# Layer 0 attention: the state behind each sequence's last chunk, and its part of the transposed k, are left out

## The chip, the cores and the metric

The kernel runs on one core of a Trainium2 chip. The metric is the device time of one execution in microseconds. Besides the timed runs there is one execution recorded by the hardware profiler; all durations below come from that recording, and its own time stands in the table further down.

A core has five engines that run beside each other and wait for each other by semaphores: TensorE (PE in the profile, with its weight loads shown apart as PEld), VectorE (DVE), ScalarE (ACT), GpSimd (POOL) and SyncE (SP), which here issues DMAs. PSUM is the memory that PE writes its results to.

## What is computed

Two blocks follow one another, each of the form x + attention(xn) * silu(ffn(xn)), on x of shape (4, 1024, 512), with xn = layernorm(x). The change is in the attention of layer 0, a linear attention with a decay per head. It runs over chunks of a sequence and carries a state S of 32 x 32 per head from chunk to chunk:

```python
def body(S, xs):
    qb, kb, vb = xs
    scores = jnp.einsum('bhid,bhjd->bhij', qb, kb) * intra_decay[None]
    o_intra = jnp.einsum('bhij,bhjd->bhid', scores, vb)
    o_inter = jnp.einsum('bhid,bhde->bhie', qb * q_decay[None, :, :, None], S)
    S_new = blk_decay[None, :, None, None] * S + jnp.einsum('bhjd,bhje->bhde', kb * k_decay[None, :, :, None], vb)
    return (S_new, o_intra + o_inter)
S0 = jnp.zeros((B, H, d, d), dtype=q.dtype)
_, o = jax.lax.scan(body, S0, (qc, kc, vc))
```

The output of a chunk reads the state in front of it (`S`). The scan's final state is thrown away (`_`). The remaining parts, which are the feed-forward network of layer 0 with ternary weights, a softmax attention with rotary positions in layer 1 and a gated feed-forward network, are not touched.

## The kernel before

The 4096 rows are eight blocks of 512 (`BLK`), so a sequence of 1024 rows is an even block and the odd block behind it. A block is four chunks of 128 rows (`TPB` = 4, `P` = 128; the kernel's chunk is twice the reference's), and the 16 heads are four groups of four heads, 128 columns each. The layer 0 attention goes through 32 steps, one for each block and group, in this order: block 0 groups 0 to 3, block 1 groups 0 to 3, and so on.

For a block and group these helpers do the work:

- `project` (matmul on L350): kT and qT, that is k and q with the group's 128 columns on the partitions and the block's 512 rows along the free axis. ACT copies each out of PSUM and adds the bias (L355), and POOL multiplies qT with its decay into qd (L357).
- `turn_k`: transposes kT chunk by chunk on PE into the PSUM tile k0t (L367), which DVE multiplies with k's decay into kd (L369).
- `states`: one matmul for each chunk, kd of the chunk with v of the chunk, into the PSUM tile u (L382). DVE copies it with a mask, which keeps the four heads apart, into slots 1 to 4 of `state[g]` (L390), and then adds to each slot the decayed slot in front of it (L395). Slot i is the state in front of chunk i. In an even block slot 0 is zero and isn't used; in an odd block POOL first copies slot 4, which the even block left, to slot 0 (L389).
- `scores`: 32 small matmuls into two large PSUM tiles sc (L408), which DVE multiplies with the decay into pt (L416).
- `outs`: state slots times qd (L432) and v times pt (L439), into the PSUM tile o, which ACT copies to oT (L445). It reads slots 0 to 3 (1 to 3 in an even block).

In step n the helpers stand on PE in this order: `scores` of step n, `project` of step n+1, a first job, `outs` of step n, `turn_k` of step n+1, in groups 0 and 1 two transposes of normalised rows of the next block (tr_x, L146), a second job, `states` of step n+1. So `turn_k` and `states` of a group are issued one step ahead. The jobs are, in groups 0 and 1, two tiles of the output projection of the block before (wo, L333, with a bias add on DVE, L338), and in groups 2 and 3 two tiles of v of the next block (v0ps, L324, with a bias add on DVE, L328). The second tile of group 3 is the fourth tile of v, which comes directly ahead of `states` of the next block's group 0. In the step before the last there are no jobs, and in the last the jobs turn rows for the feed-forward network (L457).

PE's order is kept as written. DVE, ACT, POOL and SP are ordered by a scheduler that runs when the program is built, apart from single instructions that are pinned. PSUM tiles come from a pool with two buffers for each of three kinds: k0t and tr_x share one kind (`tr`), the results of L350, L324, L333, L382 and `outs` share another (`acc`), and the tiles sc are the third. A buffer is written again when its reader has finished. Also on DVE in this stage are the statistics of the next block's rows (bn_stats and its aggregate, L105 and L108, a copy, L297, reciprocals and products, L305 to L314, with square roots on ACT, L112), and the preparation of the ternary weights (L183, L208, L210), two pieces to a step.

Of the kernel before, what the change touches and what calls it, by code (L numbers as in the profile page):

```python
# [16 lines left out]
ALU = mybir.AluOpType  # L17
AX = mybir.AxisListType

P = 128  # L20
B, N, D = 4, 1024, 512
NT = B * N
H, HD = 16, 32
# [3 lines left out]
TPB = BLK // P  # L27
# [8 lines left out]
def kernel(ctx, tc, ins, out):  # L36
# [15 lines left out]
    def acc(name):  # L52
        return psum.tile([P, 512], F32, tag="acc", name=name)

    def tr(name):
        return psum.tile([P, 4, P], F32, tag="tr", name=name)
# [177 lines left out]
    with ExitStack() as es:  # L234
# [35 lines left out]
        bdmask = wp.tile([P, P], F32, tag="bdmask", name="bdmask")  # L270
# [11 lines left out]
        kdec = wp.tile([P, H], F32, tag="kdec", name="kdec")  # L282
# [58 lines left out]
        def project(blk, g):  # L341
# [18 lines left out]
            )  # L360
            return qT, kT, qd

        def turn_k(blk, g, kT):
            nm = f"{blk}_{g}"
            kps = tr(f"k0t_{nm}")
            for i in range(TPB):
                nc.tensor.transpose(kps[:, i, :], kT[:, i * P : (i + 1) * P], ident)  # L367
            kd = p2.tile([P, TPB, P], F32, tag="kd", name=f"kd0_{nm}", bufs=1)
            nc.vector.tensor_tensor(  # L369
                kd.rearrange("p c (r d) -> p c r d", d=HD),  # L370
                kps.rearrange("p c (r d) -> p c r d", d=HD),
                kdec[:, None, 4 * g : 4 * g + 4, None].to_broadcast([P, TPB, 4, HD]),
                ALU.mult,
            )
            return kd

        def states(blk, g, kd):
            nm = f"{blk}_{g}"
            v = vs[blk]
            u = acc(f"u0_{nm}")  # L380
            for i in range(TPB):
                nc.tensor.matmul(  # L382
                    u[:, i * P : (i + 1) * P], lhsT=kd[:, i, :], rhs=v[:, i, g * P : (g + 1) * P],
                    start=True, stop=True,
                )
            s = state[g]
            fresh = blk % 2 == 0
            if not fresh:
                nc.gpsimd.tensor_copy(s[:, 0, :], s[:, TPB, :])  # L389
            nc.vector.tensor_tensor(  # L390
                s[:, 1:, :], u.rearrange("p (c e) -> p c e", e=P),
                bdmask[:, None, :].to_broadcast([P, TPB, P]), ALU.mult,
            )
            for i in range(1 if fresh else 0, TPB):
                nc.vector.scalar_tensor_tensor(  # L395
                    s[:, i + 1, :], s[:, i, :], blkdec[:, g : g + 1], s[:, i + 1, :],
                    ALU.mult, ALU.add,
                )
# [95 lines left out]
        for i in range(TPB):  # L494
            values(0, i)
        states(0, 0, turn_k(0, 0, cur[1]))
        load_x(1)
        beside = weights0()
        steps = [(blk, g) for blk in range(NBLK) for g in range(4)]
        for n, (blk, g) in enumerate(steps):  # L500
# [19 lines left out]
            if nxt:  # L520
                kd = turn_k(*steps[n + 1], nxt[1])
# [7 lines left out]
            if nxt:  # L529
                states(*steps[n + 1], kd)  # L530
# [15 lines left out]
    with ExitStack() as es:  # L546
# [143 lines left out]
        for g in range(NH0 * NBLK + 2 + 2 * TPB):  # L690
            blk, c = divmod(g, NH0)
# [115 lines left out]
    with ExitStack() as es:  # L807
# [276 lines left out]
        for s in range(TB * nu + LAG + 1):  # L1084
# [4 lines left out]
            e = s - LAG  # L1089
            if s % (2 * TB) == 0 and s < TB * nu:  # L1090

                assert not must
                n = s // (2 * TB) + 1
                if n < 4 * B:
                    b, g = divmod(n, 4)
# [23 lines left out]
            if s < TB * nu:  # L1119
                u, j = divmod(s, TB)  # L1120
# [12 lines left out]
            if 1 <= e <= TB * nu:  # L1133
                u, kb = divmod(e - 1, TB)
# [18 lines left out]
            elif s % TB == (6 if s >= TB * nu else 4) and 0 <= zu < nu - 1:  # L1153
# [3 lines left out]
                b, g, qh = units[zu]  # L1157
# [328 lines left out]
```

## Time and profile before

| what | us |
|---|---|
| median of 3 runs | 3150.0 (3148.52 to 3150.66) |
| the profiled execution | 3149.29 |
| its span, first to last instruction | 3147.5 |
| mean TensorE clock granted over the span | 0.994 of full speed |
| kT x128 transposes (L367), busy on PE | 20.9 |
| u, 128 matmuls in 256 instructions (L382), busy on PE | 35.8 |
| kd x32 (L369), busy on DVE | 22.1 |
| masked copy of u x32 (L390), busy on DVE | 22.1 |
| state updates x112 (L395), busy on DVE | 39.4 |

The layer 0 attention fills the span from its start to about 630 us, where the first matmul of the feed-forward network (L588) begins. A row of a group of instructions gives the source line, the engine, what is written from what, the number of instructions, the busy total, the mean duration of one and the idle time of the engine just ahead of them with the engine and line that ended it. A row of the timeline gives the start and the length of a run of like instructions. The end of a matmul in such a row is modelled, and instructions of one engine may overlap in it, so that the distance from one start to the next is not the duration. In a list of the chain of waits, "issue" is time in which an engine waited for nothing that the profile shows.

### The profile page before, as it was taken

The page shows a single profiled execution, that of the slowest core. Times are in us where ns is not written, and L with a number is a line of the kernel's source. Part 1 is how long each engine was busy: PE and PEld are TensorE (multiplying, and loading weights), DVE is VectorE, ACT ScalarE, POOL GpSimd, SP SyncE. Part 2 cuts the span into 40 slices and gives each one's busy share as a digit, 9 for nine tenths or more (in the row PEclk, how much of TensorE's full clock was granted, in tenths as well). Part 3 has the DMA queues.
Part 4 walks back from the last instruction along what each step waited for, and adds up shares of the span by engine and source line. Part 5 has one row for each costly group of instructions (what it writes and reads, how often), then busy time and mean ns, then how long its engine had stood idle before and what let it go on. Part 6 is the DMA issues. An engine that isn't in the chain of part 4 may idle for free.

```text
span 3147.5 us, 61092 instructions
## 1 busy us (share of the span) xinstructions
PE 3088.4 (98%) x26233; PEld 1765.4 (56%) x26233; DVE 1905.1 (61%) x2638; ACT 1196.1 (38%) x1696; POOL 1501.4 (48%) x615
## 2 busy tenths in 40 slices
PE   9999999999999998999999999999999999999998
PEld 5555555578777874443344444334444435888887
DVE  4444555468888775656656555555555684566655
ACT  3111111155555542444444444444444444333332
POOL 0000000034444344898888988888888970000001
PEclk9999999999999999999999999999999999999999
DMA  3111111122222231100001000010000013322211
GB/s 131 54 54 54 54 57 44 38 64 91 81 81 71 94 138 38 48 9 8 8 17 40 12 12 15 20 35 14 10 17 15 12 44 100 119 75 66 67 51 55
DMA packets 97799, 158.46 MB, mean 50 GB/s; under 512 B 13040, under 2 KB 26864, under 8 KB 97392
## 3 DMA queue, kind: packets, MB, share of 16 engines
q1 hardware_dynamic: 96704, 151.33, 15.5%
q8 instruction: 207, 3.39, 0.5%
q0 software_dynamic: 816, 3.15, 0.3%
q14 instruction: 72, 0.59, 0.1%
HBM read 104.10 MB, written 41.94 MB: 46 GB/s over the span
## 4 chain that ended last, share of the span: by engine, by line
PE 84%; DVE 11%; issue 2%; ACT 2%; POOL 1%; SPq 1%; DMA 0%; ACTq 0%; POOLq 0%; DVEq 0%
PE sk L1027 9%; PE sq L1000 8%; PE y L1046 8%; PE qk L350 7%; PE gate L1218 5%; PE up L1218 5%; PE dn L1240 5%; PE v1ps L856 4%; PE v0ps L324 3%; PE wo L333 3%; PE wo L856 3%; PE wq L856 3%; PE fc L588 3%; PE wk L856 3%; PE pj L641 3%; PE sk L1033 2%
## 5 line engine op out<-in xcount | busy, mean ns | idle before, releaser
L1067 POOL TENSOR_TENSOR part<-part,pT 128x2048 f32<-128x2048 f32 x184 | 844.8, 4591 | 25.7 <-ACT pT L1038 16.5
L1004 DVE TENSOR_REDUCE mx<-sq 128x2 f32<-128x1024 f32 x512 | 603.3, 1218 | 384.3 <-PE sq L1000 383.1
L1038 ACT ACTIVATE pT<-sk 128x1024 f32<-128x1024 f32 x512 | 496.3, 1021 | 619.4 <-PE sk L1033 616.1
L1027 PE MATMUL sk<-wqT,wkT 32*128 32x512 f32 x2048 | 332.5, 645 | 4.3 <-DVE mx L1004 4.3
L1000 PE MATMUL sq<-wkT,wqT 32*128 32x512 f32 x2048 | 322.5, 641 | 6.1 <-ACT pT L1038 5.1
L1046 PE MATMUL y<-pT,v 128*32 128x512 f32 x2048 | 276.3, 610 | 0.2 <-ACT pT L1038 0.2
L609 POOL TENSOR_TENSOR sums<-sums,h 128x512 f32<-128x512 f32 x112 | 162.9, 1455 | 228.9 <-ACT h L593 223.8
L641 PE MATMUL pj<-wpj,hp 128*128 128x512 f32 x1024 | 265.2, 397 | 5.8 <-DVE hp L601 4.9
L588 PE MATMUL fc<-xp,wfc 128*128 128x512 f32 x1024 | 261.1, 397 | 2.9 <-ACT h L593 2.0
L1262 POOL TENSOR_TENSOR th<-th,x 128x512 f32<-128x512 f32 x31 | 40.1, 1295 | 457.9 <-DVE th L1261 377.0
L1033 PE MATMUL sk<-mT,onesr 2*128 2x512 f32 x1024 | 239.3, 788 | 2.2 <-DVE mT L1016 2.2
L357 POOL TENSOR_TENSOR qd<-qT,wqkv 128x512 f32<-128x512 f32 x32 | 41.1, 1285 | 405.0 <-ACT qT L355 379.1
L350 PE MATMUL qk<-xnT,wqkv 128*128 128x512 f32 x512 | 230.0, 602 | 0.7 <-ACT xnT L148 0.7
L641 PEld LDWEIGHTS pj<-wpj,hp 128*128 128x128 f32 x1024 | 190.0, 188 | 58.2 <-DVE hp L601 17.4
L588 PEld LDWEIGHTS fc<-xp,wfc 128*128 128x128 f32 x1024 | 187.3, 188 | 44.4 <-ACT h L593 5.0
L1027 PEld LDWEIGHTS sk<-wqT,wkT 32*128 32x128 f32 x2048 | 99.9, 184 | 138.0 <-issue 111.4
L1218 PE MATMUL gate<-xp,wf 128*128 128x512 f32 x704 | 174.1, 389 | 0.0
L1065 POOL TENSOR_TENSOR part<-pT,pT 128x2048 f32<-128x2048 f32 x31 | 141.2, 4555 | 69.0 <-ACT pT L1038 68.8
L1218 PE MATMUL up<-xp,wf 128*128 128x512 f32 x704 | 173.8, 389 | 0.0
L1240 PE MATMUL dn<-wf,hp 128*128 128x512 f32 x704 | 173.5, 389 | 0.0
L601 DVE TENSOR_TENSOR hp<-h,hp 128x512 fp32r<-128x512 f32 x128 | 116.9, 913 | 76.2 <-ACT hp L598 76.1
L350 PEld LDWEIGHTS qk<-xnT,wqkv 128*128 128x128 f32 x512 | 95.2, 191 | 112.8 <-issue 104.2
(219 smaller groups left out, 4543.4 us busy)
## 6 DMA issues: line engine op xcount, KB each, us to landing
s<-s SPq DMA_DIRECT2D x96, 256.0 KB
x<-x SPq DMA_DIRECT2D x36, 256.0 KB
x<-in_x SPq DMA_DIRECT2D x32, 256.0 KB
raw_fc<-in_w_fcT SPq DMA_DIRECT2D x32, 256.0 KB
x0f<-in_x SPq DMA_DIRECT2D x32, 256.0 KB
x0r<-in_x SPq DMA_DIRECT2D x32, 256.0 KB
x<-th SPq DMA_DIRECT2D x32, 256.0 KB
xnT<-xnT_d SPq DMA_DIRECT2D x8, 1024.0 KB
```

What stands on the lines that cost most here:

```text
L350: nc.tensor.matmul(a, lhsT=wqkv[k][:, c0 : c0 + P], rhs=xnTs[blk][:, k, :], start=(k == 0), stop=(k == KD - 1),)
L588: nc.tensor.matmul(a, lhsT=wfc[k][:, c * P : (c + 1) * P], rhs=xp[n][:, k, :].bitcast(F32R), start=(k == 0 and n == 0), stop=(k == KD - 1 ...
L641: nc.tensor.matmul(ds[i], lhsT=hparts[blk, c][n][:, i * P : (i + 1) * P], rhs=wpj[c], start=(c == 0 and n == 0), stop=(c == NH0 - 1 and n ...
L856: nc.tensor.matmul(out[r0 : r0 + HD, :], lhsT=lhsT[:, r0 : r0 + HD], rhs=rhs, start=start, stop=stop,)
L1000: nc.tensor.matmul(sq[:, hh, :], lhsT=qT[r, q0 : q0 + P], rhs=kT[r, n * 512 : (n + 1) * 512], start=True, stop=True,)
L1004: nc.vector.tensor_reduce(mx[:, qt, 2 * pair : 2 * pair + 2, n], sq, AX.X, ALU.max)
L1027: nc.tensor.matmul(sks[h // 2][:, h % 2, :], lhsT=kT[r, kb * P : (kb + 1) * P], rhs=qT[r, qh * 512 : (qh + 1) * 512], start=True, stop=False,)
L1038: nc.scalar.activation(pT[:, 2 * pair : 2 * pair + 2, :], sks[pair], AF.Exp, scale=QKS)
L1046: nc.tensor.matmul(y[r, :], lhsT=v[:, kb, r], rhs=pT[:, h, :], start=(kb == 0), stop=(kb == TB - 1),)
L1067: add.tensor_tensor(parts[u], parts[u], pT, ALU.add)
L1218: nc.tensor.matmul(a, lhsT=ws[n, c][:, k, :], rhs=xp[m][:, k, :], start=(k == 0 and m == 0), stop=(k == KD - 1 and m == 1),)
L1240: nc.tensor.matmul(ds[i], lhsT=hparts[blk, c][n][:, i * P : (i + 1) * P], rhs=w, start=(c == 0 and n == 0), stop=(c == NH1 - 1 and n == 1),)
```

## The change

In odd blocks the fourth chunk is left out of `turn_k` and of `states`: the chunk isn't transposed, kd, the masked copy and the matmuls cover three chunks, and the update of slot 4 is gone. Slot 4 of an odd block is the state behind the sequence's last chunk. Even blocks are as before.

```diff
+        def used(blk):
+
+            return TPB if blk % 2 == 0 else TPB - 1
+
         def turn_k(blk, g, kT):
             nm = f"{blk}_{g}"
             kps = tr(f"k0t_{nm}")
-            for i in range(TPB):
+            n = used(blk)
+            for i in range(n):
                 nc.tensor.transpose(kps[:, i, :], kT[:, i * P : (i + 1) * P], ident)
             kd = p2.tile([P, TPB, P], F32, tag="kd", name=f"kd0_{nm}", bufs=1)
             nc.vector.tensor_tensor(
-                kd.rearrange("p c (r d) -> p c r d", d=HD),
-                kps.rearrange("p c (r d) -> p c r d", d=HD),
-                kdec[:, None, 4 * g : 4 * g + 4, None].to_broadcast([P, TPB, 4, HD]),
+                kd[:, :n].rearrange("p c (r d) -> p c r d", d=HD),
+                kps[:, :n].rearrange("p c (r d) -> p c r d", d=HD),
+                kdec[:, None, 4 * g : 4 * g + 4, None].to_broadcast([P, n, 4, HD]),
                 ALU.mult,
             )
             return kd
...
             u = acc(f"u0_{nm}")
-            for i in range(TPB):
+            n = used(blk)
+            for i in range(n):
                 nc.tensor.matmul(
                     u[:, i * P : (i + 1) * P], lhsT=kd[:, i, :], rhs=v[:, i, g * P : (g + 1) * P],
                     start=True, stop=True,
...
             nc.vector.tensor_tensor(
-                s[:, 1:, :], u.rearrange("p (c e) -> p c e", e=P),
-                bdmask[:, None, :].to_broadcast([P, TPB, P]), ALU.mult,
+                s[:, 1 : n + 1, :], u[:, : n * P].rearrange("p (c e) -> p c e", e=P),
+                bdmask[:, None, :].to_broadcast([P, n, P]), ALU.mult,
             )
-            for i in range(1 if fresh else 0, TPB):
+            for i in range(1 if fresh else 0, n):
                 nc.vector.scalar_tensor_tensor(
                     s[:, i + 1, :], s[:, i, :], blkdec[:, g : g + 1], s[:, i + 1, :],
                     ALU.mult, ALU.add,
```

## The prediction

> **What bounds the kernel now.** First the busy shares of the page and the chain of work that ended last:
>
> ```profile
> PE 3088.4 (98%) x26233; PEld 1765.4 (56%) x26233; DVE 1905.1 (61%) x2638; ACT 1196.1 (38%) x1696; POOL 1501.4 (48%) x615
> PE 84%; DVE 11%; issue 2%; ACT 2%; POOL 1%; SPq 1%; DMA 0%; ACTq 0%; POOLq 0%; DVEq 0%
> ```
>
> TensorE (PE) carries the end. A share over the whole run says nothing of one stage, so next the busy times of the stretch that holds the layer 0 attention, 60 to 640 us (columns: length, then busy time and instruction count of PE, weight loads, DVE, ACT, POOL, then clock, DMA share, GB/s):
>
> ```profile
> 60.00:640.00 580.00, 571.01 (x3598) 320.67 (x3596) 283.04 (x558) 84.13 (x140) 44.19 (x46) 1.00 0.17 53
> ```
>
> PE 98%, DVE 49%, clock full, DMA a sixth. So work taken from PE's queue here is gained, and work taken from DVE only where PE waits for it. Then the groups that the change touches (busy total, mean ns of one, idle before it):
>
> ```profile
> L367 PE MATMUL k0t<-ident,kT 128*128 128x128 f32 x128 | 20.9, 286 | 0.0
> L382 PE MATMUL u<-v,kd 128*128 128x128 f32 x256 | 35.8, 278 | 2.6 <-DVE kd L369 1.8
> L369 DVE TENSOR_TENSOR kd<-k0t,kdec 128x512 f32<-128x512 f32 x32 | 22.1, 691 | 57.1 <-PE k0t L367 57.1
> ```
>
> A matmul of u is two instructions (256 for 128 matmuls). Last the timeline of PE over two steps, block 1 group 0 and group 1 (start, length, then the idle time before it):
>
> ```profile
> 94.08 0.66 PE L367 MATMUL k0t<-ident,kT 128*128 128x128 f32 x4
> 94.57 3.60 PE L324 MATMUL v0ps<-wqkv,xnT 128*128 128x512 f32 x8
> 98.00 1.43 PE L382 MATMUL u<-v,kd 128*128 128x128 f32 x8
> 99.37 1.17 PE L408 MATMUL sc<-qT,kT 32*128 32x128 f32 x32
> ...
> 112.87 0.66 PE L367 MATMUL k0t<-ident,kT 128*128 128x128 f32 x4
> 113.36 0.60 PE L146 MATMUL tr_x<-ident,xn 128*128 128x128 f32 x4
> 114.31 0.66 PE L146 MATMUL tr_x<-ident,xn 128*128 128x128 f32 x4 [0.35 <-DVE kd L369]
> 114.80 3.60 PE L333 MATMUL wo<-wout,oT 128*128 128x512 f32 x8
> 118.24 1.05 PE L382 MATMUL u<-v,kd 128*128 128x128 f32 x8
> 119.22 1.17 PE L408 MATMUL sc<-qT,kT 32*128 32x128 f32 x32
> ```
>
> Read the starts, not the lengths: from one group's start to the next's is what a group costs the queue. Four transposes cost 94.57 - 94.08 = 0.49 us, 0.1225 each; eight u instructions 119.22 - 118.24 = 0.98 us, 0.1225 each, but 1.37 us in group 0.
>
> **The change part by part.** It acts in blocks 1, 3, 5, 7, all four groups: 16 steps. In the built program's order each of these has three transposes and six u instructions instead of four and eight, and the DVE forms of kd and of the state mask are 128x384 with three instead of four state updates.
>
> *Transposes.* 16 x 0.1225 = 1.96 us off PE's queue. Here a rule counts otherwise: the Trainium skill, "TensorE: Matmul & The Clock Gate", Part 4, puts a 128x128 transpose at about 275 ns inside a kernel (bf16). The trace's duration is the same kind of number (286 ns mean), yet four start within 0.49 us. By the rule's figure the sum would be 16 x 0.275 = 4.4 us, by the starts 1.96. I take the starts: a queue advances by them.
>
> *u.* 16 x 2 x 0.1225 = 3.92 us, by the same reading.
>
> *A wait in group 0.* In blocks 1, 3, 5, 7 the u group of group 0 takes 1.37 us (starts 98.00, 250.96, 404.36, 557.32), 0.39 more than eight instructions. The weight-load timeline shows it ahead of the last two:
>
> ```profile
> 98.95 0.30 PEld L382 LDWEIGHTS u<-v,kd 128*128 128x128 f32 x2 [0.31 <-DVE v L328]
> ```
>
> The fourth chunk's u needs the fourth tile of v, whose bias add on DVE (0.69 us) has just begun. That u goes, and with it the wait: the next reader of that tile is outs, 11 us later. 4 x 0.39 = 1.56 us. What is late next there: the projection needs the same add for its PSUM buffer, but only after 1.10 us of scores. The add ends at about 98.8, the scores then at 99.7: covered.
>
> *A wait in groups 1 and 2.* The second tr_x waits for kd, which frees the PSUM buffer of k0t: its start lies 114.31 - 113.36 = 0.95 us after the first's, 0.46 over the 0.49 of four transposes. kd on 384 columns: the trace has no such row. If time went with columns it would lose 0.173 us of 0.692; a 128x4 tensor_tensor takes 0.16, so most of it is a fixed part, and (0.692 - 0.16) / 508 x 128 = 0.134. I take 0.134, since 384 is near 512 and the fixed part is measured; 0.173 stays as the upper end. The wait stays above zero, so all of it is gained, in blocks 1, 3, 5, two steps each: 6 x 0.134 = 0.80 us.
>
> *The last step, block 7 group 3,* has no projection behind it, and DVE is on the chain:
>
> ```profile
> 606.28 0.70 DVE kd L369
> 606.99 0.14 issue
> 607.12 1.14 PE u L382 x8
> 608.36 0.70 DVE state L390
> ...
> 610.25 0.35 DVE state L395
> 610.60 2.39 DVE pt L416 x4
> ```
>
> Beside the 0.37 already counted, kd gives 0.134, the mask (L390) 0.134, and a state update (L395) 0.38 (they start 0.38 apart): 0.65 us. The pt then start about 1.0 us earlier; the scores they need end at 609.28, 0.5 earlier with the change, so DVE stays last.
>
> *Elsewhere* the shorter mask and the missing update (together 0.51 us of DVE, 15 times) buy nothing: outs follows the scores by 11.5 us. If that cover were gone they would be worth up to 7.7 us more.
>
> *What moves.* DVE's order is the scheduler's, and in group 0 of blocks 1, 3 and 5 the first pt now stands behind three bn_stats instead of two, and ACT has the square root of the next block's variance ahead of the copy of kT instead of behind it. One bn_stats and its aggregate are 0.67 us. Before, the pt end at about 106.9 and outs reads them at 111.9 (less 0.8 now): 4 us of cover, cost nothing. The ACT swap is a new wait: the root waits for DVE's copy (L297). From the starts of the rows I get DVE free for bn_stats at 100.4 (101.7 before), the copy at 105.2, the root at 105.4, kT from 105.6 to 106.3. Queued behind it: the second root, qT, and PE's wo, which takes kT's PSUM buffer. PE wants that buffer at 107.44 - 0.76 = 106.7, its weight load at 106.3. So the cover is 0 to 0.4 us. I take nothing; if my sum of DVE is 0.5 us short, it costs 3 x 0.5 = 1.5 us. No gain is possible there, as kT was in time before. On SP one x load moves ahead of one weight load in block 5; both are wanted a step or more later: nothing. POOL's order is unchanged, and so is everything after the attention.
>
> *Sum.* 1.96 + 3.92 + 1.56 + 0.80 + 0.65 = 8.9 us. Downstream every instruction keeps its place and PE is released by PE or DVE, so the shift is carried to the end. The profiled execution took 3149.3 us (span 3147.5): 3140.4. The median of the runs is 3150.0, 0.7 above it: **3141.1 us**.
>
> **The rivals.**
>
> *A new wait takes the place.* The kT copy comes late and wo waits about 1 us in three steps: 8.9 - 3.0 = 5.9 saved, 3144.1, no change to be told. For it: the cover above is thin. Against: two of the terms would have to be wrong by 0.6 us in rows that repeat to 0.01.
>
> *Durations are the price.* If each removed instruction freed its whole length, 16 x 0.286 + 32 x 0.278 = 13.5 us, with the waits 16.5: 3133.5. Against: the starts.
>
> *The clock.* The Trainium skill, same page, Part 1, says that the gate halves TensorE's clock after an idle window of about 3.4 us, and that the window runs free of the kernel. The rows: clock 0.66 in 2540 to 2560, 0.83 in 2600 to 2620, where the tail of the layer 1 attention waits for DVE. By the rule a shift of 8.9 us is a new phase, a matter of luck; 0.83 over 20 us is 0.17 x 20 = 3.4 us of full clock lost, the most that one such stretch can cost. The change ends slower only from three such stretches more, by over 0.2% from five (17 - 8.9 = 8.1: 3158). By the rows, three executions of before, each with its own phase, lie within 2.1 us, so I expect 1 us of scatter, not 15.
>
> That the change doesn't do what it says is excluded by the program's order.
>
> **How the numbers follow.** About 0.2% (6.3 us) can be told from no change here. My forecast 0.80, the new wait 0.10, durations 0.05, the clock 0.05 (of which slower by over 0.2%: 0.03). The forecast with its bounds (7.4 to 9.3 saved) and the runs' scatter is 3139.5 to 3143.5; the range reaches to the new wait and part of the way to the durations: 3137.5 to 3144.6. Nearly all of the forecast and the durations are faster, 0.83; the rest of them, the new wait and a small clock loss are the same, 0.14; slower 0.03.
>
> **What would show it.** The start of sc 0.74 us after u in group 0 of the odd blocks (1.37 before) and no wait for v there; tr_x's wait 0.33 instead of 0.46; kd and the mask at 0.56; pt in the last step about 1.0 us earlier against its k0t; the layer 0 attention 8.9 us shorter, and everything behind it as long as before. Wrong would be a wait of wo (L333) for ACT in three steps, or a stretch behind 640 us that is longer by as much as this one is shorter.

## The result, and the profile after

| | before | after | ratio after / before, 95% interval |
|---|---|---|---|
| 8 runs of each | 3150.33 us (3146.57 to 3153.89) | 3141.93 us (3137.86 to 3147.13) | 0.9972 (0.9962 to 0.9981) |
| the profiled execution's span | 3147.5 | 3141.6 | |

The change makes the kernel 8.4 us faster by the medians, 0.28%. The interval reaches from 6 to 12 us, because single executions of either kernel scatter by 7 to 9 us. The page of the changed kernel, busy shares and chain:

```profile
span 3141.6 us, 60980 instructions
PE 3083.5 (98%) x26185; PEld 1762.0 (56%) x26185; DVE 1898.5 (60%) x2622; ACT 1195.6 (38%) x1696; POOL 1501.6 (48%) x615
PE 84%; DVE 11%; ACT 2%; issue 2%; POOL 1%; SPq 1%; DMA 0%; ACTq 0%; POOLq 0%; DVEq 0%
```

PE has 48 instructions less (16 transposes, 32 of u), DVE 16 less, and PE still carries the end. Its lines from `turn_k` on have moved: L367 is now L372, L382 is L388, L369 is L374, L390 is L396, L395 is L401, L408 is L414, and lines further down are 6 higher. The groups, over the first 640 us:

```profile
L388 PE MATMUL u<-v,kd 128*128 128x128 f32 x224 | 31.1, 277 | 2.0 <-DVE kd L374 1.7
L372 PE MATMUL k0t<-ident,kT 128*128 128x128 f32 x112 | 19.2, 288 | 0.0
L396 DVE TENSOR_TENSOR state<-u,bdmask 128x384 f32<-128x384 f32 x16 | 8.9, 558 | 1.1 <-PE u L388 1.1
L374 DVE TENSOR_TENSOR kd<-k0t,kdec 128x384 f32<-128x384 f32 x16 | 8.9, 557 | 29.8 <-PE k0t L372 29.8
```

The forms on 384 columns take 0.557 us, 0.135 less than the 0.692 on 512. The same two steps on PE, block 1 groups 0 and 1:

```profile
93.93 0.55 PE L372 MATMUL k0t<-ident,kT 128*128 128x128 f32 x3
94.32 3.60 PE L324 MATMUL v0ps<-wqkv,xnT 128*128 128x512 f32 x8
97.75 0.83 PE L388 MATMUL u<-v,kd 128*128 128x128 f32 x6
98.51 1.17 PE L414 MATMUL sc<-qT,kT 32*128 32x128 f32 x32
...
106.59 3.60 PE L333 MATMUL wo<-wout,oT 128*128 128x512 f32 x8
...
112.02 0.55 PE L372 MATMUL k0t<-ident,kT 128*128 128x128 f32 x3
112.40 0.60 PE L146 MATMUL tr_x<-ident,xn 128*128 128x128 f32 x4
113.21 0.66 PE L146 MATMUL tr_x<-ident,xn 128*128 128x128 f32 x4 [0.21 <-DVE kd L374]
113.71 3.60 PE L333 MATMUL wo<-wout,oT 128*128 128x512 f32 x8
117.14 0.83 PE L388 MATMUL u<-v,kd 128*128 128x128 f32 x6
117.90 1.17 PE L414 MATMUL sc<-qT,kT 32*128 32x128 f32 x32
```

Take the starts again. The transposes cost 0.38 to 0.39 us (0.49 before), u 0.76 in both steps (1.37 and 0.98), and from tr_x to tr_x it is 0.81 (0.95). Going through all 32 steps, the changed kernel is ahead of the other by 0.14 us at the start, and each odd block adds 0.71 us in group 0, 0.47 in groups 1 and 2 and 0.33 in group 3 (block 7, without tr_x: 0.71, 0.33, 0.33). Even blocks add nothing. Between the last transposes and the feed-forward network the last step adds 1.0 us, and the first matmul of the feed-forward network starts at 622.05 instead of 630.49: 8.44 us earlier, 8.30 without the start.

The rest of the program has the same instructions in the same order, so the lead should stay 8.4. It is 8.7 us at the end of the feed-forward network, 9.3 at 1880 us, 8.0 at 1910, 4.4 at 2162 and 6.1 from 2611 us to the end. The profiled pair thus shows 5.9 us, though the stage that was changed gave 8.3. What took the difference is the last question below.

### The profile page after: what moved, and what is told of

It is laid out like the page before. It is cut to its first block, busy times and chain, and to the rows that moved or that the text cites. A ratio compares the mean times of both kernels' runs of the same rounds, so it can differ in the third digit from the quotient of the medians.

```text
span 3141.6 us, 60980 instructions
## 1 busy us (share of the span) xinstructions
PE 3083.5 (98%) x26185; PEld 1762.0 (56%) x26185; DVE 1898.5 (60%) x2622; ACT 1195.6 (38%) x1696; POOL 1501.6 (48%) x615
## 4 chain that ended last, share of the span: by engine, by line
PE 84%; DVE 11%; ACT 2%; issue 2%; POOL 1%; SPq 1%; DMA 0%; ACTq 0%; POOLq 0%; DVEq 0%
PE sk L1033 9%; PE sq L1006 8%; PE y L1052 8%; PE qk L350 7%; PE gate L1224 5%; PE up L1224 5%; PE dn L1246 5%; PE v1ps L862 4%; PE v0ps L324 4%; PE wo L333 3%; PE wo L862 3%; PE wk L862 3%; PE wq L862 3%; PE fc L594 3%; PE pj L647 3%; PE sk L1039 2%
## 5 line engine op out<-in xcount | busy, mean ns | idle before, releaser
L350 PE MATMUL qk<-xnT,wqkv 128*128 128x512 f32 x512 | 229.9, 602 | 0.7 <-ACT xnT L148 0.7
L350 PEld LDWEIGHTS qk<-xnT,wqkv 128*128 128x128 f32 x512 | 95.5, 191 | 112.4 <-issue 106.3
```

What stands on the lines that cost most here:

```text
L350: nc.tensor.matmul(a, lhsT=wqkv[k][:, c0 : c0 + P], rhs=xnTs[blk][:, k, :], start=(k == 0), stop=(k == KD - 1),)
```

## The experiments

To compare one stage across executions I take these spans from each trace: the layer 0 attention from the first matmul of the second step's projection (L350) to the first of the feed-forward network (L588 before); the feed-forward network from there to the start of its last matmul (L641); the layer 1 attention from its first sq (L1000, q times k, from which DVE takes the maxima of the softmax) to its last y (L1046, the weights times v). The first span leaves out the loads at the start of the program, which vary by 3 us. The last column is the time within the layer 1 attention in which the granted clock of TensorE was 0.50. A version for which no time is given below was run once and is judged by these spans alone. All times in us.

| kernel | layer 0 attention | against before | layer 0 feed-forward | layer 1 attention | half clock in it |
|---|---|---|---|---|---|
| before | 592.32 | | 533.29 | 1431.25 | 20.5 |
| after | 584.02 | -8.30 | 532.99 | 1433.98 | 23.9 |
| after, again | 584.01 | -8.31 | 533.13 | 1430.22 | 13.7 |
| only u, mask and updates cut | 586.70 | -5.62 | 534.46 | 1431.12 | 17.1 |
| only transposes and kd cut | 589.62 | -2.70 | 534.59 | 1434.74 | 23.9 |
| only the wait on v gone | 590.78 | -1.54 | 532.88 | 1433.15 | 20.5 |
| only mask and updates cut | 591.76 | -0.56 | 532.89 | 1432.80 | 17.1 |
| one more chunk cut | 577.25 | -15.07 | 533.01 | 1434.37 | 23.9 |
| second tr_x put later | 578.04 | -14.28 | 534.67 | 1425.07 | 6.8 |
| before, mT from PSUM | 592.31 | -0.01 | 532.93 | 1440.04 | 20.5 |
| after, mT from PSUM | 584.03 | -8.29 | 532.96 | 1442.82 | 20.5 |

The first column repeats to 0.02 us for the same code (592.32 and 592.31; 584.02, 584.01 and 584.03), and in none of the eleven traces does a stretch of half clock fall into it, so one trace is enough to settle a tenth of a microsecond there.

**Only u.** The changed kernel, with the transposes and kd of before.

```diff
         def turn_k(blk, g, kT):
...
-            n = used(blk)
+            n = TPB
```

> The transposes and kd stay at four chunks in every block; u, the mask and the state updates of odd blocks cover three, so slot 4 of odd blocks is left out. Read at the first matmul of the feed-forward network of layer 0 (630.49 us in the trace of before). My theory, with the costs of the changed kernel's trace (0.22 us for two u instructions, 0.39 for the wait on v, 0.51 in the last step): 16 x 0.22 + 4 x 0.39 + 0.51 = 5.6 us earlier. Rival, the wait on v only moves to the projection behind it, which needs the same add: 4.0. Rival, instructions count by their durations: 32 x 0.278 + 2.1 = 11.

5.62 us: as expected, and neither rival (4.0 or 11).

**Only the transposes.** The changed kernel again, but the fourth u stays and reads the third kd.

```diff
-            n = used(blk)
+            n = TPB
             for i in range(n):
                 nc.tensor.matmul(
-                    u[:, i * P : (i + 1) * P], lhsT=kd[:, i, :], rhs=v[:, i, g * P : (g + 1) * P],
+                    u[:, i * P : (i + 1) * P], lhsT=kd[:, min(i, used(blk) - 1), :], rhs=v[:, i, g * P : (g + 1) * P],
```

> Only the transposes and kd of odd blocks cover three chunks; the fourth u takes the third chunk's kd in place of its own, with the fourth tile of v as before, so that u, its wait, the mask and the state updates stay (slot 4 of odd blocks then holds another state, which nothing reads). My theory: 16 x 0.107 + 6 x 0.134 (second tr_x behind kd) + 0.134 (last step) = 2.65 us earlier at the first matmul of the feed-forward network. Rival, kd is hidden anyway: 1.7. With the run in which only u is cut it should sum to the change's 8.3.

2.70 us against 2.65, not the rival's 1.7: the shorter kd is worth the 0.9 expected of it (0.80 ahead of tr_x, 0.13 in the last step). The two parts sum to 8.32, the change to 8.30: they don't hide each other.

**Only the wait.** The kernel before, with another operand in the fourth u of odd blocks.

```diff
-                    u[:, i * P : (i + 1) * P], lhsT=kd[:, i, :], rhs=v[:, i, g * P : (g + 1) * P],
+                    u[:, i * P : (i + 1) * P], lhsT=kd[:, i, :], rhs=v[:, min(i, TPB - 1 - blk % 2), g * P : (g + 1) * P],
```

> All the work of before, but in odd blocks the fourth u reads the third tile of v instead of the fourth (slot 4 of odd blocks then holds another state, which nothing reads). So nothing goes but the wait of group 0 on the bias add of v. My theory: 4 x 0.39 = 1.56 us earlier at the first matmul of the feed-forward network, and the wait is gone from the weight loads of u in blocks 1, 3, 5, 7. Rival, absorbed by the scores or the projection behind: 0.

1.54 us with no instruction less. The timeline of PE in this kernel, block 1 group 0:

```profile
96.24 1.05 PE L382 MATMUL u<-v,kd 128*128 128x128 f32 x8
97.22 1.17 PE L408 MATMUL sc<-qT,kT 32*128 32x128 f32 x32
98.33 7.13 PE L350 MATMUL qk<-xnT,wqkv 128*128 128x512 f32 x16
```

Eight instructions now cost 97.22 - 96.24 = 0.98 us, as in every other group, and qk follows the scores at the usual 1.11. Of the seven waits of u on v (2.1 us over the stage) three are left (0.9 us), those of the even blocks. So 1.5 of the change's 8.3 us come from which tile is read, not from how much is computed.

**Only DVE.** The kernel before, with the shorter mask and one update less.

```diff
+            n = TPB if fresh else TPB - 1
...
-                s[:, 1:, :], u.rearrange("p (c e) -> p c e", e=P),
-                bdmask[:, None, :].to_broadcast([P, TPB, P]), ALU.mult,
+                s[:, 1 : n + 1, :], u[:, : n * P].rearrange("p (c e) -> p c e", e=P),
+                bdmask[:, None, :].to_broadcast([P, n, P]), ALU.mult,
             )
-            for i in range(1 if fresh else 0, TPB):
+            for i in range(1 if fresh else 0, n):
```

> TensorE's work is that of before; only the mask and the state updates of odd blocks are cut to three chunks (slot 4 is left out). DVE has 0.51 us less in each of 16 steps. My theory: it is hidden in 15 of them and shows in the last step alone, 0.51 us earlier at the first matmul of the feed-forward network. Rival, DVE bounds the steps: up to 16 x 0.51 = 8.2.

0.56 us, not 8.2: that is one step's share (0.51 expected), so the work of the mask and the updates is hidden in 15 of the 16 steps.

**One more chunk.** A second cut of the same size shows what a chunk costs without the wait. This version leaves out a state that `outs` needs, so only its times are of use.

```diff
-            return TPB if blk % 2 == 0 else TPB - 1
+            return TPB if blk % 2 == 0 else TPB - 2
```

> The changed kernel with one chunk less again in odd blocks: the state in front of the last chunk is left out too, which outs reads (it then reads an older one). A second step of the same size without the wait on v. By the costs of the changed kernel's trace: 16 x (0.107 + 0.22) + 6 x 0.134 + 0.65 = 6.7 us earlier than the changed kernel at the first matmul of the feed-forward network. By the costs of the forecast (0.1225 an instruction): 5.88 + 1.45 = 7.3. If the rest of a step becomes the bound, less than 5.

584.02 - 577.25 = 6.77 us: the costs of the changed kernel's trace (6.7), not those of the forecast (7.3). PE stays the bound. Block 1 group 0 again:

```profile
92.47 0.44 PE L372 MATMUL k0t<-ident,kT 128*128 128x128 f32 x2
92.75 3.60 PE L324 MATMUL v0ps<-wqkv,xnT 128*128 128x512 f32 x8
96.18 0.61 PE L388 MATMUL u<-v,kd 128*128 128x128 f32 x4
96.72 1.17 PE L414 MATMUL sc<-qT,kT 32*128 32x128 f32 x32
```

Two, three and four transposes cost 0.28, 0.39 and 0.49 us; four, six and eight u instructions 0.54, 0.76 and 0.98. Each instruction is 0.11 us, and a group costs 0.06 to 0.10 more that doesn't depend on its length.

**The tail: mT.** This pair asks what gave back part of the lead behind 1880 us. In the profiled pair the largest step lies at the same mT in both kernels (mx are the maxima of the softmax of layer 1; mT holds them transposed, and DVE makes it from two copies by ACT, mf and the rounded mh). Before, and then after, timeline of DVE:

```profile
2152.39 0.75 DVE L1016 SCALAR_TENSOR_TENSOR mT<-mh,second,mf 128x512 fp32r<-128x512 f32 x1 [0.50 <-ACT mh L1014]
2155.35 2.36 DVE L1004 TENSOR_REDUCE mx<-sq 128x2 f32<-128x1024 f32 x2 [2.21 <-PE sq L1000]
```

```profile
2144.42 5.13 DVE L1022 SCALAR_TENSOR_TENSOR mT<-mh,second,mf 128x512 fp32r<-128x512 f32 x1 [0.50 <-ACT mh L1020]
2149.47 2.34 DVE L1010 TENSOR_REDUCE mx<-sq 128x2 f32<-128x1024 f32 x2
```

The same instruction takes 0.75 us in one and 5.13 in the other, and behind it the maxima (mx) come late for PE, after:

```profile
2150.74 0.70 PE L1033 MATMUL sk<-wqT,wkT 32*128 32x512 f32 x2 [0.91 <-DVE mx L1010]
```

An addition of GpSimd begins 0.050 us after mT's start in the first trace (and takes 5.1 us) and 0.025 us after it in the second (4.6 us). In this, before is the exception: in each of the eight other traces without the edit below an addition begins 0.025 to 0.042 us after an mT, and this mT takes 5.12 to 5.14 us. The experiment takes one operand of mT from PSUM, in both kernels:

```diff
-                mTs[u], mh.bitcast(F32), second, mf, ALU.mult, ALU.add
+                mTs[u], mh.bitcast(F32), second, tp, ALU.mult, ALU.add
```

> The changed kernel, with one operand changed in layer 1: mT (L1022) takes the transposed maxima from PSUM, where TensorE left them, instead of from their copy in SBUF; the values are the same. In the traces mT takes 0.74 us when GpSimd adds nothing at its start and up to 5.13 us when an addition of GpSimd is under way or begins within about 0.03 us. My theory: with one operand in PSUM, mT no longer waits for GpSimd's addition, all 32 take under 1 us, layer 1's attention has fewer half-clock stretches and the kernel is 10 to 30 us faster than before, with less scatter between runs. Rival, mT waits for GpSimd whatever its operands are: long mT remain and the time is that of the changed kernel, about 3142.

> The kernel before with the same operand of mT taken from PSUM, nothing else. It is the pair of the run with the changed kernel: if the part given back behind 1890 us came from mT and the clock, the two differ by the whole gain of the layer 0 attention, 8.3 to 8.9 us, with less scatter than the original pair, in which single runs spread over 7 to 9 us. Rival, the given back part is an effect of the change itself: they differ by 6.

Half of this theory fell. All 32 mT take 0.735 to 0.750 us in the changed kernel with this edit (0.740 to 5.131 without), so the wait for GpSimd is gone. But nothing of the 10 to 30 us came: against before, 3152.7 us in this set (25 executions), the kernel with the change took 3150.83 us (3147.82 to 3156.32, ratio 0.9996, interval 0.9986 to 1.0006), and the one without took 3161.55 (ratio 1.0029, 1.0018 to 1.0040). Both are thus some 9 us slower than they are without the edit. The layer 1 attention takes 1443 and 1440 us, longer than in every other trace, and its half clock, 20.5 us in both, did not become less either. PE's waits there, in the changed kernel with this edit:

```profile
PE wo L862 <- DVE mT L1022: 8.5, 12, 0.8
PE wk L862 <- DVE mT L1022: 4.8, 6, 0.8
PE v1ps L862 <- DVE mT L1022: 3.5, 4, 2.3
PE wq L862 <- DVE mT L1022: 3.4, 8, 0.4
```

20 us of new waits: mT now holds the only PSUM buffer of its kind until ACT's second copy and mT itself are done, and the next projection wants it. The waits on mx that went were 5.1 us in the changed kernel and are 1.1 here. As a pair the two kernels with the edit differ by 10.7 us at the medians and 8.28 in the layer 0 attention; the layer 1 attention scatters by 3 us between them as well, so they give no narrower answer than the first pair.

**Again.**

> The changed kernel once more, on the chip of the run before it and with more runs. My theory: the layer 0 attention takes 584.0 us to within 0.05 us as in the first trace, and the time is 8.5 us under before, within what the layer 1 attention scatters (its stage took 1431 to 1435 us in seven traces of the same instructions). Rival, part of the gain is lost for good behind layer 0: 6 us or less.

3139.58 us (3135.43 to 3144.72, 7 runs) against 3152.19 (3141.78 to 3156.66, 12 runs), ratio 0.9964 (0.9950 to 0.9978). That is 12.6 us where 8.5 were expected; the interval, about 7 to 16 us, holds 8.5 and not the rival's 6. The layer 0 attention took 584.01 us. The profiled span was 3139.3, 2.3 under the first one of the same kernel: the layer 1 attention was 3.8 shorter (1430.22 instead of 1433.98), the start of the program 1.5 longer. So nothing is lost for good behind layer 0.

**A wait removed.** The trace after still has PE wait for kd ahead of the second tr_x. This version lets the second wo tile pass in front of it.

```diff
-                for i in range(2):
-                    turn0(blk + 1, 2 * g + i)
+                turn0(blk + 1, 2 * g)
+                if jobs:
+                    jobs[1][0](*jobs[1][1:])
+                turn0(blk + 1, 2 * g + 1)
                 if g == 1 and blk + 2 < NBLK:
                     load_x(blk + 2)
-            if jobs:
+            elif jobs:
                 jobs[1][0](*jobs[1][1:])
```

> The changed kernel with the second tr_x of groups 0 and 1 put behind the second job (the second wo tile) on TensorE, so that kd, which frees its PSUM buffer, is done by then. The wait that the change shortened from 0.46 to 0.33 us in odd blocks goes altogether, and so does the 0.46 of even blocks; block 0 has no second job and keeps its two. My theory: 6 x 0.33 + 6 x 0.46 = 4.7 us earlier at the first matmul of the feed-forward network than the changed kernel, and about as much in the time, about 13 us under before. Rival, a new wait takes the place (the mask of u is now behind the second xn on DVE, which waits for the first tr_x): under 1 us.

The layer 0 attention takes 578.04 us, 5.98 less than the changed kernel (4.7 expected), and the time is 3132.90 us (3128.56 to 3137.30, 6 runs), 6.7 under the changed kernel of the same set (3139.58). Against before it is 19.3 us by the medians, where about 13 were expected, ratio 0.9947 (0.9933 to 0.9961). PE in block 1 group 1:

```profile
110.44 0.55 PE L372 MATMUL k0t<-ident,kT 128*128 128x128 f32 x3
110.83 0.60 PE L146 MATMUL tr_x<-ident,xn 128*128 128x128 f32 x4
111.26 3.60 PE L333 MATMUL wo<-wout,oT 128*128 128x512 f32 x8
114.70 0.60 PE L146 MATMUL tr_x<-ident,xn 128*128 128x128 f32 x4
115.14 0.83 PE L388 MATMUL u<-v,kd 128*128 128x128 f32 x6
```

The first tr_x costs 0.43 us and the second 0.44, 0.87 together. In the changed kernel they cost 113.71 - 112.40 = 1.31. That is 0.44 less where I had counted 0.33: placed apart, each group is also 0.06 us cheaper than the 0.49 I had taken as its cost. Why, no run shows.

## Why the prediction was right

The forecast was 8.9 us off the profiled execution's time and 3141.1 us; the median came out at 3141.93, and the stage that was changed gave 8.30. That the medians differ by nearly the same, 8.4, is luck in part: their interval reaches from 6 to 12, and the second set gave 12.6. What bears the forecast out is the stage and its parts. By its own steps:

- *Transposes*, forecast 1.96 us: 16 x 0.108 = 1.7. *u*, forecast 3.92: 16 x 0.22 = 3.5. Here lies nearly all that the sum is off (0.6 us): I divided a whole group's distance by its instructions, 0.49 / 4 and 0.98 / 8, and so counted with each instruction a share of what a group costs whatever its length. The step from two to three to four shows 0.11 each. The rule of about 275 ns for a transpose (the Trainium skill, "TensorE: Matmul & The Clock Gate", Part 4) was further off than the 0.1225 of the forecast, as a price of a place in the queue: by duration the transposes agree with it (288 ns on average in the changed kernel).
- *The wait on v*, forecast 1.56: 1.54 by itself, with all work kept. The scores and the projection behind did not take it back. (The add of v ended at 98.89, from its row at 98.20 and 0.69 long, not at 98.8; the cover stays.)
- *kd ahead of the second tr_x*, forecast 6 x 0.134: the distance from tr_x to tr_x fell from 0.95 to 0.81, and cutting the transposes and kd alone gave 2.70, which is 16 x 0.108 + 7 x 0.135 within 0.03. The estimate of 0.558 us for 384 columns from the fixed part was right (0.557), and 0.173 less in proportion would have been wrong.
- *The last step*, forecast 0.65 beyond the instructions: 1.00 us from the last transposes on, less 0.33, gives 0.67. It is the one place where DVE's part counts, and DVE alone gave 0.56 for mask and update (forecast 0.51).
- *Elsewhere DVE's savings buy nothing*: shown by the same run.
- *The swapped order on ACT costs nothing*: DVE's copy, ACT's root and kT, and the weight load of wo in the changed kernel, block 1 group 0:

```profile
105.03 0.16 DVE L297 COPY st<-st 128x4 f32<-128x4 f32 x1
```

```profile
105.22 0.30 ACT L112 ACTIVATE st<-st,eps 128x4 f32<-128x4 f32 x1 [10.57 <-DVE st L297]
105.43 0.67 ACT L355 ACTIVATE kT<-qk,bqk 128x512 f32<-128x512 f32 x1
```

```profile
106.16 0.19 PEld L333 LDWEIGHTS wo<-wout,oT 128*128 128x128 f32 x1 [0.24 <-ACT kT L355]
```

  kT is copied from 105.43 to 106.10, where the forecast had 105.6 to 106.3, and wo starts at 106.59 straight behind qk, as before the change. The gain of group 0 is 0.71 in each of blocks 1, 3 and 5, the sum of its parts (0.11 + 0.22 + 0.39) to 0.01, so the rival of a new wait is out. It was a near thing: kT was done 0.06 us ahead of wo's weight load and 0.49 ahead of its first matmul, where the forecast had 0 to 0.4. That it held is in part luck.
- *The durations as price*, 16.5 us: out, by the stage (8.30) and by each part.
- *Downstream the shift is carried to the end*: right for the layer 0 feed-forward network (lead 8.44 at its start, 8.74 at its end), and not to better than some microseconds behind it. The forecast took the scatter of before, 2.1 us in three runs, for the scatter of this kernel and expected 1 us, "not 15"; more runs spread over 7 to 16 us (3142.51 to 3158.08 in the largest set of 25). It also took 3.4 us of full clock for the most that one stretch can cost. Its own row of 2540 to 2560 says 6.8 (0.34 x 20): the clock is halved there from 2541.8 for 13.7 us.

**What sets the scatter** is mostly the clock. In the nine traces without the edit of mT, the layer 1 attention, whose instructions and order on PE are the same in all, took 1425.07 to 1434.74 us. By the last column of the table it took 1425.07 with 6.8 us of half clock, 1430.22 with 13.7, 1431.12 and 1432.80 with 17.1, 1431.25 and 1433.15 with 20.5, and 1433.98 to 1434.74 with 23.9. Less half of that time, the nine lie between 1421.0 and 1424.3: a spread of 3.3 us instead of 9.7. Whole executions go the same way. In the set of 25, the two with a mean clock of 0.997 took 3142.51 and 3144.39 us, the seven with 0.992 took 3149.84 to 3158.08, and 0.005 of 3147 us is 15.7 us of full clock. Of the 2.7 us that the profiled pair lost in the layer 1 attention (1433.98 against 1431.25), 1.7 are thus 3.4 us more of half clock, and PE's waits for mx, 5.1 us instead of 4.3, come to another 0.8.

At the largest step of the lead both meet, in the changed kernel:

```profile
2148.60:2152.00 3.40, 2.49 (x16) 0.79 (x12) 3.21 (x3) 0.01 (x1) 3.32 (x2) 1.00 0.00 0
2152.00:2155.40 3.40, 3.40 (x30) 1.51 (x32) 0.00 (x0) 2.44 (x3) 3.26 (x2) 0.50 0.00 0
```

(Busy PE, weight loads, DVE, ACT, POOL, then the clock.) PE lacks 0.91 us of work in the first stretch, waiting for mx behind the long mT, and has half its clock in the second. The lead falls from 8.0 to 4.4 us around here. That mT's wait for GpSimd brings on such stretches is argued, not shown: with the edit that ended this wait both kernels still had 20.5 us of half clock, but the edit brought a new wait, and no version free of both was tried.

## What to carry to other kernels

Price an instruction that goes by the distance between starts, and take that distance from two groups of different length, so that what a group costs once doesn't enter. Look at what the dropped instruction waited for, and at who waited for the one that only gets shorter: here they held 1.5 and 0.9 of 8.3 us, and moving a single transpose group out of such a wait gave another 6. A gain of 0.3% in one stage can be proved in a stage that repeats to 0.02 us while the kernel's own time scatters by ten; compare stages. Where a stage does scatter, set its time beside the half clock in it before looking for another cause.

## What the runs showed of the hardware

The half-clock stretches in these traces start whole multiples of 3.41 us apart (in before, 2541.81 and 2603.25 us: 18 times) and last 3.4, 6.8 or 13.7 us, but for the last, which the end of the recording cuts. This fits the free-running window of the Trainium skill ("TensorE: Matmul & The Clock Gate", Part 1). But they did not need an idle window of that length. Of those in the layer 1 attention, several follow 3.4 us in which PE's idle time adds up to 0.6 to 0.9 us (0.63 at 1882 us and 0.91 at 2152 us in the changed kernel). Nor does idle time alone decide: in the feed-forward network of before, PE was idle for 1.88 of the 3.40 us from 650.80 (such a window by the count of multiples), and the clock stayed full. What the limit is stays open. The layer 0 feed-forward network shows the cost of one stretch at 637 to 648 us: the three traces that have it took 534.5 to 534.7 us, the other eight 532.9 to 533.3, so about 1.6 us, close to half of 3.4.

A scalar_tensor_tensor on DVE with all operands in SBUF (mT) waited for an addition of GpSimd that began up to 0.042 us after it (5.12 to 5.14 us instead of 0.75, eight traces), and not for one that began 0.050 us after it; there the addition took 5.1 us instead of 4.6. Every mT of over 1 us in the nine traces ended 0.54 to 0.56 us behind the end of an addition. With one operand in PSUM none of 64 took more than 0.750.
